# Layer 2 of a four-layer graph network: VectorE adds the four node chunks of a block's norm, and TensorE's sum over nodes takes one product per block

## The chip, the cores and the metric

The kernel runs on one core of a Trainium2 chip. The metric is the device time of one execution in microseconds, from the median of several runs. The profile is of one execution; its page and its trace give times in microseconds from the start of the span.

## The reference, cut to what matters

The program passes x, 8 batches of 2048 nodes with 64 features, through four layers. Each layer normalises its input over the features, takes the positive part h, and adds the layer's result on h to x:

```
h = maximum(layernorm(x), 0)
x = x + layer(h, adj)
```

Layers 0, 1 and 2 multiply h by the 2048 x 2048 matrix `adj` (once or more) and by small weights. Layer 3 is an attention over nodes whose scores are masked with `adj > 0.5`:

```
att = where(adj > 0.5, e, -9e15)
out = elu(einsum('bij,bjc->bic', softmax(att, axis=2), h))
```

Each row of `adj` is 0/1 divided by the row's sum, so with the given data an entry is usually far below 0.5, the mask is empty in every row, the softmax is uniform, and layer 3 is the mean of h over all nodes, through `elu`, added to x. The kernel computes this uniform case, tests on the way that the data allow it, and branches to a general path at the end if they don't. So for the last two layers, what is computed is: layer 2's result, added to x; its norm h; the sum of h over 2048 nodes for each batch and feature; `elu` of that sum divided by 2048, added to x.

## The kernel before, in words

The batches are taken in four pairs p. A pair's two batches lie side by side, so that a tile has 2 x 64 = 128 features. The nodes are taken in four blocks nb of 512, a block being four chunks of 128 nodes: a node block is a tile of 128 partitions by 4 chunks by 128 features. In layer 2 the blocks of all pairs are counted through as g = 4p + nb, from 0 to 15.

For each g, `product` (line 245) multiplies h, split into a high and a low half (tiles H and L), by the transposed pattern of `adj` (tile BT): 16 steps m of two matmuls each, into a bank of PSUM. VectorE then scales the bank into the tile e (`scaled`, line 240). The work of earlier blocks is hung between the steps of the product by the dictionary `fill`, whose keys are steps:

- at step 5, `behind(g)`: `finish2(g - 1)` multiplies e of block g - 1 by the layer's weights (`bn`, line 665), adds it to x (line 941, tile acc) and starts that block's norm;
- at step 12, `go_on`: the next stage of the norms that are under way;
- behind step 15, `sums(g - 2)`: TensorE multiplies a matrix of ones by the norm z of block g - 2, which sums z over its nodes (line 949, `pS`). Four products per block, one for each chunk, and all 16 products of a pair add up in one bank.

The norm (`norm_stages`, lines 174 to 200) goes over three engines: VectorE takes the mean and subtracts it (179 to 181), ScalarE squares (186), VectorE sums the squares (189, 191), GpSimd takes the power -1/2 (194), VectorE scales and takes the positive part (197). Then `done(h)` is called, which in layer 2 keeps z for `sums`.

After a pair's last block, `outputs` (from line 957) divides by the number of nodes, takes `elu` (960 to 963), adds it to the pair's four kept blocks (966) and stores them. Besides, `prepare_next` loads the next pair's h and splits it into H (ScalarE, line 230) and L (VectorE, line 232).

Behind the last product, `layer2` finishes block 15: `finish2(15)`, `sums(14)`, the rest of the norm, `sums(15)`, outputs.

The order of instructions on each engine is fixed when the kernel is built, by a planner that takes them in program order and moves some of them by its estimate of when their inputs are ready. Engines meet through semaphores.

Of the kernel before, what the change touches and what calls it, by code (L numbers as in the profile page):

```python
# [8 lines left out]
F32 = mybir.dt.float32  # L9
# [5 lines left out]
ALU = mybir.AluOpType  # L15
AX = mybir.AxisListType
# [26 lines left out]
def uniform_path(  # L43
# [30 lines left out]
    nc = tc.nc  # L74
    P = 128
    B, N, C = x.shape
    NP = B // 2
    NCH = N // P
    NB = N // 512
# [21 lines left out]
    def bank(tag, name):  # L101
        return psums[-1].tile([P, 512], F32, tag=tag, name=name)
# [11 lines left out]
    ones = consts.tile([P, P], F32, name="ones")  # L114
# [19 lines left out]
    def nodes(acc):  # L134

        return acc.rearrange("p j f -> p (j f)").rearrange("p (e j c) -> p j e c", e=2, c=C)
# [6 lines left out]
    def fill_x(acc, layer, p, nb, queue=nc.sync):  # L143
        if layer == 0:
            return queue.dma_start(runs(acc), runs_of(x, p, nb))
        return queue.dma_start(acc, xs[p][:, part(nb), :])
# [14 lines left out]
    def split(t):  # L161
        return t.rearrange("p j (b c) -> p j b c", b=2)
# [11 lines left out]
    def norm_stages(xt, name, done, out_):  # L174

        z = block("z", f"z_{name}", 3)
        g = groups(z)
        mean = small.tile([P, 8], F32, name="mean")
        nc.vector.tensor_reduce(each(mean), nodes(xt), axis=AX.X, op=ALU.add)
        nc.vector.tensor_scalar(mean, mean, 1.0 / C, None, op0=ALU.mult)  # L180
        firsts.append(nc.vector.tensor_tensor(  # L181
            split(z), nodes(xt), each(mean)[:, :, :, None].to_broadcast([P, 4, 2, C]),
            op=ALU.subtract
        ))
        sq = block("sq", f"sq_{name}", 1)
        squares.append(nc.scalar.activation(sq, z, AF.Square))  # L186
        yield
        var = small.tile([P, 8], F32, name="var", bufs=3)
        nc.vector.tensor_reduce(var, groups(sq), axis=AX.X, op=ALU.add)  # L189
        variances.append(  # L190
            nc.vector.tensor_scalar(var, var, 1.0 / C, EPS, op0=ALU.mult, op1=ALU.add)  # L191
        )
        rstd = small.tile([P, 8], F32, name="rstd", bufs=3)
        powers.append(nc.gpsimd.tensor_tensor(rstd, var, mhalf, op=ALU.pow))  # L194
        yield
        h = z if out_ is None else out_
        scales.append(nc.vector.scalar_tensor_tensor(  # L197
            groups(h), g, 0.0, rstd[:, :, None].to_broadcast([P, 8, C]), op0=ALU.max, op1=ALU.mult
        ))
        done(h)  # L200
        yield

    def norm_relu(xt, name, done, out_=None):
        n = norm_stages(xt, name, done, out_)
        next(n)
        pending.append([n, 2])
# [16 lines left out]
    lastp = []  # L223
# [52 lines left out]
    def term(k, name):  # L276
        pool = l0t if k == 1 else l0f[0]
        return pool.tile([P, 512], F32, tag=f"t{k}", name=name, bufs=(2, 4, 1)[k])
# [289 lines left out]
    for m in range(NCH):  # L568
        if m in (2, 7, 12):
            go_back(1 + m // 5)  # L570
        for i in range(2):
            nc.tensor.matmul(
                ps, hls[1][m // 4][i][:, m % 4, :], BT[:, m, 3 * 512:],
                start=(m == 0 and i == 0), stop=(m == NCH - 1 and i == 1),
# [80 lines left out]
    def feat(i, name):  # L655

        if i == 0:
            return term(1, name)
        return lastp[0].tile([P, 512], F32, tag="fm", name=name, bufs=4)

    def back_to_nodes(fT, wmat, name, tag="big"):

        ps = psums[-1].tile([P, 4, 2 * C], F32, tag=tag, name=f"bn_{name}")
        for t in range(4):
            nc.tensor.matmul(ps[:, t, :], fT[:, t * P:(t + 1) * P], wmat, start=True, stop=True)  # L665
        return ps
# [264 lines left out]
    accs, es, zs, pS = [], [], {}, {}  # L931

    def finish2(g):
        p, nb = divmod(g, NB)
        nm = f"acc_2_{p}_{nb}"
        acc = term(1, nm) if p % 2 else feat(1, nm)
        acc = acc.rearrange("p (j f) -> p j f", j=4)
        accs.append(acc)
        fill_x(acc, 2, p, nb)
        pn = back_to_nodes(es[g], wos, f"2_{p}_{nb}")  # L940
        nc.vector.tensor_tensor(nodes(acc), split(pn), nodes(acc), op=ALU.add)
        norm_relu(acc, f"3_{p}_{nb}", lambda h: zs.update({g: h}))

    def sums(g):
        p, nb = divmod(g, NB)
        if nb == 0:
            pS[p] = bank("tr", f"pS_{p}")
        for t in range(4):
            nc.tensor.matmul(  # L949
                pS[p][:, :2 * C], ones, zs[g][:, t, :],  # L950
                start=(nb == 0 and t == 0), stop=(nb == NB - 1 and t == 3),
            )
        if nb == NB - 1:
            outputs(p)

    def outputs(p):

        y = lastp[0].tile([P, 2 * C], F32, name="y")
        ex = lastp[0].tile([P, 2 * C], F32, name="ex")
        nc.vector.tensor_scalar(y, pS[p][:, :2 * C], 1.0 / N, None, op0=ALU.mult)  # L960
        nc.scalar.activation(ex, y, AF.Exp)
        nc.vector.tensor_scalar(ex, ex, 1.0, -1.0, op0=ALU.min, op1=ALU.add)
        nc.vector.scalar_tensor_tensor(y, y, 0.0, ex, op0=ALU.max, op1=ALU.add)
        for nb in range(NB):
            acc = accs[NB * p + nb]
            nc.vector.tensor_tensor(nodes(acc), nodes(acc), rows4(y), op=ALU.add)
            queue = nc.scalar if nb % 2 == 0 and p == NP - 1 else nc.sync
            queue.dma_start(runs_of(out, p, nb), runs(acc))

    def layer2(n, p):  # L970
        hl, _ = ops[n]

        def behind(g):
            go_on()
            if g > 0:
                finish2(g - 1)
            if g % NB > 1:
                prepare_next(n + 1, g % NB - 2)

        for nb in range(NB):  # L980
            g = NB * p + nb
            nm = f"2_{p}_{nb}"
            crow = load_crow(nb, nm)
            fill = {5: lambda: behind(g)}
            if g > 0:
                fill[12] = go_on
            if nb == 3:
                fill[8] = lambda: prepare_next(n + 1, 2)
            if g == 1:
                fill[9] = lambda: put_off.pop()()  # L990
            if g > 1:
                fill[15] = lambda: sums(g - 2)
            e = lastp[0].tile([P, 512], F32, tag="st", name=f"e_{nm}", bufs=3)
            es.append(product(hl, nb, nm, e, crow, fill=fill))
            if g == 0:
                go_on()
        prepare_next(n + 1, 3)
        if p == NP - 1:
            go_on()
            finish2(g)  # L1000
            sums(g - 1)
            all_done()
            sums(g)
# [600 lines left out]
```

## Time and profile before

The time before is 1248.38 us, the median of 3 runs (1244.74 to 1248.88). The profiled execution has a span of 1245.5 us.

| what | from the page or the trace |
|---|---|
| TensorE matmul busy | 1211.7 us, 97% of the span |
| VectorE busy | 745.5 us, 60% |
| ScalarE, GpSimd busy | 181.7 us (15%), 223.9 us (18%) |
| chain that ended last, by engine | TensorE 93%, DMA 3%, VectorE 3%, GpSimd 1% |
| `pS`, line 949: matmul records | 128, median 275 ns, from 1107.3 to 1235.6 us |
| granted TensorE clock, mean of the span | 0.994 |
| 1160 to 1170 us (layer 2, a block without outputs): VectorE busy | 4.97 of 10 us |
| 1170 to 1180 us (layer 2, a block with outputs): VectorE busy | 7.54 of 10 us |
| both of these: TensorE matmul busy | 10.00 of 10 us |

The page's chain is the way back from the last instruction, at each step to what released it or, where nothing did, to the instruction before it on its engine. An engine's share of the chain says how much of the end it set; its busy time alone doesn't. A product in 32-bit floats appears as two matmul records in the trace, so the four products of one block's sum are eight records. Matmuls overlap in the records (275 ns each, though eight of them take 0.89 us in the chain), so lengths on TensorE are read from the chain or from starts. TensorE is PE in the profile, its weight loads PEld, VectorE is DVE, ScalarE ACT, GpSimd POOL.

### The profile page before, as it was taken

To read this page: it belongs to the slowest core of one execution; us is meant where nothing else is said; L and a number is where in the kernel's file an instruction comes from. 1 tells how busy PE (TensorE), PEld (TensorE's weight loads), DVE (VectorE), ACT (ScalarE), POOL (GpSimd) and SP (SyncE) were. 2 spreads that over 40 slices of the span, in tenths; PEclk is the share of its full clock that TensorE was granted. 3 is DMA by queue.
4 is the path that set the end of the run, shared out by engine and by line. 5 is a ranking of instruction groups with operands and counts; after the bars stand their busy time and mean duration, and the time that the engine had idled before them with its cause. 6 is when DMAs were issued, how large, how long until landed. Compare 5 with 4: busy or idle time off the path is not lost.

```text
span 1245.5 us, 15336 instructions
## 1 busy us (share of the span) xinstructions
PE 1211.7 (97%) x5702; PEld 860.6 (69%) x5702; DVE 745.5 (60%) x1940; ACT 181.7 (15%) x281; POOL 223.9 (18%) x233
## 2 busy tenths in 40 slices
PE   5999999999999999999999999999999999999995
PEld 4775555555665557655577888788788878888884
DVE  5356888777757774477654445445543545566664
ACT  6610001000010000000111121112111211211100
POOL 5410222211131111011110022003101300231211
PEclk9999999999999999999999999999999999999998
DMA  9951334332332232122265436533643553433311
GB/s 358 372 142 53 101 107 115 85 87 72 90 106 67 65 89 79 51 64 64 60 148 135 110 100 153 116 90 119 161 106 90 152 127 96 128 137 117 115 56 46
DMA packets 100984, 140.98 MB, mean 113 GB/s; under 512 B 43772, under 2 KB 58108, under 8 KB 98852
## 3 DMA queue, kind: packets, MB, share of 16 engines
q1 hardware_dynamic: 82820, 80.74, 24.8%
q0 software_dynamic: 11776, 48.15, 13.0%
q10 hardware_dynamic: 6304, 11.01, 2.7%
q8 instruction: 47, 0.77, 0.2%
q14 instruction: 37, 0.30, 0.1%
HBM read 95.03 MB, written 35.66 MB: 105 GB/s over the span
## 4 chain that ended last, share of the span: by engine, by line
PE 93%; DMA 3%; DVE 3%; POOL 1%; issue 0%; ACT 0%; SPq 0%; POOLq 0%; ACTq 0%
PE bv L250 38%; PE y L711 26%; PE bn L665 5%; PE ph L900 3%; PE bv_2b L250 2%; PE bv_1b L250 2%; PE bv_3b L250 2%; PE bv_0b L250 2%; DMA BT<-in_adj_dram 2%; PE bn_u L665 1%; PE bv_0a L250 1%; PE bv_3a L250 1%; PE pt L262 1%; PE bv_2a L250 1%; PE pS L949 1%; PE bv_1a L250 1%
## 5 line engine op out<-in xcount | busy, mean ns | idle before, releaser
L250 PE MATMUL bv<-BT,H 128*128 128x512 f32 x1024 | 426.3, 416 | 0.0
L250 PE MATMUL bv<-BT,L 128*128 128x512 f32 x1024 | 401.0, 392 | 0.0
L250 PEld LDWEIGHTS bv<-BT,H 128*128 128x128 f32 x1024 | 192.5, 188 | 47.8 <-issue 11.6
L250 PEld LDWEIGHTS bv<-BT,L 128*128 128x128 f32 x1024 | 192.7, 188 | 47.5 <-issue 11.5
L720 DVE SCALAR_TENSOR_TENSOR acc<-y,emb,acc 128x128 f32<-128x128 f32 x512 | 176.2, 344 | 65.7 <-PE y L711 65.7
L720 DVE SCALAR_TENSOR_TENSOR odd<-y,emb,odd 128x128 f32<-128x128 f32 x448 | 153.3, 342 | 0.0
L711 PE MATMUL y<-wt,t0T 64*128 64x512 f32 x512 | 143.7, 607 | 2.4 <-DVE odd L720 1.7
L240 DVE TENSOR_TENSOR g<-bv,crow 128x512 f32<-128x512 f32 x48 | 33.2, 692 | 183.2 <-PE bv L250 183.2
L194 POOL TENSOR_TENSOR rstd<-var,mhalf 128x8 f32<-128x8 f32 x64 | 105.7, 1653 | 180.6 <-DVE var L191 174.8
L186 ACT ACTIVATE sq<-z 128x512 f32<-128x512 f32 x64 | 40.4, 631 | 406.6 <-DVE z L181 396.6
L711 PEld LDWEIGHTS y<-wt,t0T 64*128 64x128 f32 x512 | 45.8, 185 | 63.3 <-issue 57.1
L692 POOL TENSOR_TENSOR acc<-acc,b2r 128x512 f32<-128x512 f32 x16 | 22.2, 1389 | 315.5 <-DVE z L181 315.5
L692 POOL TENSOR_TENSOR acc<-acc,wl 128x512 f32<-128x512 f32 x16 | 20.7, 1291 | 299.3 <-DVE z L181 299.2
L711 PE MATMUL y<-wt,t1T 64*128 64x512 f32 x256 | 66.8, 589 | 0.0
L197 DVE SCALAR_TENSOR_TENSOR z<-z,rstd 128x512 f32<-128x512 f32 x64 | 44.7, 703 | 35.5 <-POOL rstd L194 35.5
L665 PEld LDWEIGHTS bn<-wl,g 128*128 128x128 f32 x384 | 49.5, 191 | 5.1 <-ACT g L905 1.5
L189 DVE TENSOR_REDUCE var<-sq 128x8 f32<-128x512 f32 x64 | 43.6, 681 | 15.6 <-ACT sq L186 15.6
L665 PE MATMUL bn<-wl,g 128*128 128x128 f32 x384 | 51.1, 276 | 0.0
L846 DVE SCALAR_TENSOR_TENSOR junk<-mt,cols,st 128x512 uint8<-128x512 bf16 x64 | 47.7, 745 | 4.1 <-DMA mt<-MD 3.7
L711 PEld LDWEIGHTS y<-wt,t1T 64*128 64x128 f32 x256 | 27.1, 187 | 27.8 <-issue 27.8
L905 ACT ACTIVATE g<-g,b1s 128x512 f32<-128x512 f32 x32 | 23.2, 724 | 137.2 <-DVE g L904 137.1
L691 POOL DMA_DIRECT2D hs<-z x32 | 18.6, 582 | 133.6 <-DVE z L197 97.0
(210 smaller groups left out, 1672.4 us busy)
## 6 DMA issues: line engine op xcount, KB each, us to landing
BT<-in_adj_dram POOLq DMA_DIRECT2D x16, 1024.0 KB, 19.5
crow<-crowD SPq DMA_DIRECT2D x64, 256.0 KB, 3.3
st<-in_adj_dram SPq DMA_DIRECT2D x64, 256.0 KB, 3.6
hs<-z POOLq DMA_DIRECT2D x40, 256.0 KB, 3.2
xs<-acc POOLq DMA_DIRECT2D x32, 256.0 KB, 2.4
MD<-BT POOLq DMA_DIRECT2D x16, 512.0 KB, 5.6
acc<-xs SPq DMA_DIRECT2D x32, 256.0 KB, 3.9
hb<-hs SPq DMA_DIRECT2D x28, 256.0 KB, 3.3
```

Source lines behind the costliest of these rows:

```text
L186: squares.append(nc.scalar.activation(sq, z, AF.Square))
L189: nc.vector.tensor_reduce(var, groups(sq), axis=AX.X, op=ALU.add)
L194: powers.append(nc.gpsimd.tensor_tensor(rstd, var, mhalf, op=ALU.pow))
L197: scales.append(nc.vector.scalar_tensor_tensor(groups(h), g, 0.0, rstd[:, :, None].to_broadcast([P, 8, C]), op0=ALU.max, op1=ALU.mult))
L240: ahead.append(nc.vector.tensor_tensor(to, ps.rearrange("p (q t) -> p t q", t=4), crow, op=ALU.mult))
L250: nc.tensor.matmul(ps, hl[m // 4][i][:, m % 4, :], BT[:, m, nb * 512:(nb + 1) * 512], start=(m == 0 and i == 0), stop=(m == NCH - 1 and i ...
L665: nc.tensor.matmul(ps[:, t, :], fT[:, t * P:(t + 1) * P], wmat, start=True, stop=True)
L692: nc.gpsimd.tensor_tensor(nodes(acc), nodes(acc), more, op=ALU.add)
L711: nc.tensor.matmul(y[:, bb, :], terms[k][hs_, ts], wt[hs_, k, dg * 512:(dg + 1) * 512], start=(k == 0), stop=(k == K - 1),)
L720: last = nc.vector.scalar_tensor_tensor(xj, yd, ec, old, op0=ALU.mult, op1=ALU.add)
L846: nc.vector.scalar_tensor_tensor(junk, mt, cols[:, i, :], st, op0=ALU.mult, op1=ALU.not_equal, accum_out=bad[:, i, q:q + 1],)
L900: fill[12] = lambda: nc.tensor.matmul(ph, w1v2 if s else w1vT, gT[nb], start=True, stop=True)
```

## The change

In blocks 0 to 14, VectorE adds the four chunks of z into one tile `hs4` of 128 partitions by 128 features as soon as the norm is done, and TensorE's sum takes that one tile: one product in place of four. Block 15 still gives its four chunks to TensorE. The purpose is to take work from TensorE, and to leave the last block's path as it is. The sum over nodes is the same but for the order of additions.

```
-        norm_relu(acc, f"3_{p}_{nb}", lambda h: zs.update({g: h}))
+        norm_relu(acc, f"3_{p}_{nb}", lambda h: add_chunks(g, h))
+
+    def add_chunks(g, h):
+
+        zs[g] = [h[:, t, :] for t in range(4)]
+        if g + 1 < NP * NB:
+            hs4 = lastp[0].tile([P, 2 * C], F32, name="hs4", bufs=2)
+            nc.vector.tensor_reduce(hs4, h.rearrange("p t f -> p f t"), axis=AX.X, op=ALU.add)
+            zs[g] = [hs4]
 
     def sums(g):
...
-        for t in range(4):
+        for t, z in enumerate(zs[g]):
             nc.tensor.matmul(
-                pS[p][:, :2 * C], ones, zs[g][:, t, :],
-                start=(nb == 0 and t == 0), stop=(nb == NB - 1 and t == 3),
+                pS[p][:, :2 * C], ones, z,
+                start=(nb == 0 and t == 0), stop=(nb == NB - 1 and t == len(zs[g]) - 1),
             )
```

## The prediction

> **What bounds the kernel now.** I read the page's chain by line first, then that chain in order of time over layer 2, then the timeline of VectorE alone over the same stretch, then the timeline of the last 27 us. Times inside the kernel are on the profile's clock.
>
> First, four blocks of layer 2 in the chain, in order of time (start, us, what). Each block is 12 + 20 matmuls of the large product, with the back-projection `bn` and the sum `pS` between them. The period is 1170.93 - 1161.86 = 9.07 us, made of 7.25 (32 large products at 0.227) + 0.91 (`bn`) + 0.91 (`pS`). No wait appears: TensorE bounds this stretch.
>
> ```profile
> 1161.86 0.89 PE pS L949 x8
> 1162.75 2.74 PE bv L250 x12
> 1165.49 0.89 PE bn L665 x8
> 1166.38 4.56 PE bv L250 x20
> 1170.93 0.89 PE pS L949 x8
> ```
>
> Second, VectorE in one of those blocks (start, us, then line, operation, tiles; in brackets idle time before it and its releaser). The reader is to see a serial circle: L941 takes `bn` in, its mean and centred tile go to ScalarE (0.76 us idle at L189), the variance to GpSimd (idle at L197), and only behind L197 does the next L941 stand. In a block with outputs, the next L941 is late because of L966.
>
> ```profile
> 1166.42 0.69 DVE L941 TENSOR_TENSOR acc<-bn,acc 128x512 f32<-128x512 f32 x1 [2.57 <-PE bn L665]
> ...
> 1168.07 0.69 DVE L181 TENSOR_TENSOR z<-acc,mean 128x512 f32<-128x512 f32 x1
> 1169.52 0.69 DVE L189 TENSOR_REDUCE var<-sq 128x8 f32<-128x512 f32 x1 [0.76 <-ACT sq L186]
> ...
> 1170.97 0.69 DVE L240 TENSOR_TENSOR e<-bv,crow 128x512 f32<-128x512 f32 x1 [0.56 <-PE bv L250]
> 1172.23 0.69 DVE L197 SCALAR_TENSOR_TENSOR z<-z,rstd 128x512 f32<-128x512 f32 x1 [0.56 <-POOL rstd L194]
> ...
> 1174.08 2.50 DVE L966 TENSOR_TENSOR acc<-acc,y 128x512 f32<-128x512 f32 x4
> 1176.50 0.68 DVE L941 TENSOR_TENSOR acc<-bn,acc 128x512 f32<-128x512 f32 x1
> ```
>
> Third, the tail in the chain: from 1227.35 the last block's L941, norm and sum are one serial path to the end at 1245.5, with no large product beside it.
>
> ```profile
> 1226.27 1.06 PE bn L665 x8
> 1227.33 0.02 issue
> 1227.35 0.70 DVE acc L941
> ...
> 1231.97 1.17 POOL rstd L194
> ```
>
> [...]the L941 at 1176.50 had its `bn` a microsecond earlier, and stood behind four L966.[...] No row of this trace has such a read: the reduces L179 and L189 read runs of 64 words.
>
> **The change part by part.**
>
> *Removed from TensorE.* In 15 of 16 blocks `pS` takes one product in place of four, that is 2 matmul records in place of 8. The remaining pair costs between 0.23 (a quarter of 0.91) and 0.40; the nearest pair, L861, added 0.31 (from the large product at 1081.33 to the second behind it at 1083.00 are 1.67 us, less two pitches, 0.45, and `bn`, 0.91). I take 0.27, so 0.64 per block. Blocks 0 to 12 lie in the stream: 13 x 0.64 = 8.3 us (6.6 to 8.8). Block 13's `pS` ends at 1226.27 beside the L240 of the last product (1225.41 + 0.69), for which `bn` waits anyway: 0. Block 14's lies in the tail's idle time: 0. Block 15 keeps four products.
>
> *Added to VectorE.* Fifteen reduces `hs4`, 128x128 out of 128x512, each reading four words 512 bytes apart, then stepping one word. Their length D is the unknown: 0.69 us if it reads as L189 does[...]. I take 0.69[...].
>
> *Where it stands.* In the build's order the reduce comes straight behind L197 and ahead of the next block's L941 (in two places per four blocks one or two other instructions move as well). So it is inside the circle. Behind it stand L941, then the whole norm, then L240, and TensorE's next `bn` waits for L240. The sum that reads `hs4` comes some 6 us later and waits for nothing.
>
> *The circle, worked out.* Without waits for TensorE, one turn is 1172.23 - 1166.42 = 5.81, plus the pitch of 0.61 to the next unrelated instruction: 6.42. From the L941 of block 1 (1105.28) to that of block 15 (1227.35) are 14 turns in 122.07 us. They need 14 x 6.42 = 89.9; plus the low halves L232 that lie between (ten of them, 0.6 each where visible: 2.2, 2.5 and 1.2 in the three groups of four) 5.9; plus three sets of outputs, 3.66 each now (1176.50 - 1172.84), about 3.1 in the new order, in which y is taken earlier and the exponential runs beside the reduce: 9.3; plus three places where the new order puts L240 ahead of L191, 0.6 each: 1.8. Sum 106.9, so the circle has 15.2 us to spare over the 14 turns. Each reduce takes D + 0.02 of it. The first one, in block 0, stands between L189 and L191 of layer 1's last norm at 1102.7 and moves the first L941 by D - 0.1. The last L941 moves by 14(D + 0.02) + (D - 0.1) - 15.2 = 15 D - 15.0 us. With D = 0.69 that is -4.7.
>
> *Which is later.* TensorE alone would be 8.3 us earlier, and the tail then pays block 14's reduce ahead of the last L941, +0.7: -7.6. The circle ends later, at -4.7, so it sets the end; TensorE waits for L240 in a few blocks (after product 2 first, where L240 ends only 1.0 us before `bn` starts even now: 1109.86 against 1110.89; then in the blocks with L232). The tail behind the last L941 is the same work. Buffers: z is freed earlier, the new tile has two buffers, no transfer is added: 0, all beside the products.
>
> **Forecast and rivals.** The median before is 1248.4.
> - *The reduce runs at full rate, the circle eats part of the gain* (0.48): 1248.4 - 4.7 = 1243.7.
> - *The strided read costs 1.04 us* (0.30): 15 x 1.04 - 15.0 = +0.6, that is 1249.0. The gain is turned into waits of TensorE's `bn` for L240.[...]
> - [...] (0.14): +3.0 to +6.6, at most 1255.0, slower than before; VectorE becomes the bound of layer 2.[...]
> - *TensorE stays the bound* (0.08): the circle is shorter than I summed (L232 and outputs slip into its idle time), -7.6, that is 1240.8.
>
> The range from 1240.0 to 1250.5 takes in three of the four and leaves out most of the third, some 0.15. Faster by over 0.3% (3.7 us): five sixths of the first case, as runs of one kernel scatter by 4 us (1244.74 to 1248.88), and the last: 0.40 + 0.08 = 0.48. Within 0.3%: the rest of the first, nearly all of the second, a little of the third: 0.37. Slower: 0.15.
>
> **What would show it.** Right: `hs4` rows of 0.68 to 0.70 us, 15 of them; `pS` pieces of about 0.27 in the chain; `bn` waiting for `e` of L240, about 2 us in all, first near 1110; VectorE entering the chain before 1220. D off: the `hs4` row says so at once, and each 0.1 us moves the end by 1.5. Wrong in the circle: no wait of `bn` for L240, and a period of 8.4 us throughout. Wrong on TensorE: a pair in `pS` that costs 0.5 or more.

## The result, and the profile after

In the first comparison the changed kernel took 1244.68 us (median of 4 runs, 1244.5 to 1245.27) and the kernel before 1247.76 (4 runs, 1244.74 to 1248.88): ratio 0.998, interval 0.9962 to 0.9998. In a second comparison of the same two kernels, with 13 runs against 35, it was 1245.88 against 1246.7, ratio 0.9998, interval 0.9989 to 1.0006. (The ratio is the recorded estimate from all runs; the two medians alone give 0.9993.) The first interval ends just under 1; the second, with far more runs, takes 1 in. So no gain is shown, and the second interval leaves one of 1.4 us at most (0.0011 x 1246.7).

To see where time goes inside layer 2, whole runs are too coarse, because runs of one kernel scatter by 4 to 5 us. From here on **the stretch** is the time from the first L240 of layer 2 (the `e` of block 0) to the first of the last four output additions. What follows it is the same work in every kernel. It takes 1237.28 - 1090.23 = 147.05 us before and 1235.00 - 1088.14 = 146.86 us after: 0.19 less. A second profile of the changed kernel (below) has 146.18, so two profiles of one kernel differ by up to 0.7 here, and 0.19 is within that.

The chain of waits after the change, by engine (section 4 of the page). It had 93% on TensorE before.

```profile
PE 86%; DVE 6%; DMA 3%; POOL 2%; issue 1%; ACT 1%; POOLq 0%; ACTq 0%; DVEq 0%
```

The chain of the changed kernel in order of time (start, us, what), at three places.

```profile
1123.47 0.22 PE pS L957 x2
1123.69 2.77 PE bv L250 x12
1126.46 0.89 PE bn L665 x8
1127.35 4.56 PE bv L250 x20
1131.91 0.22 PE pS L957 x2
...
1152.33 0.61 DVE var L189
...
1153.04 0.70 DVE e L240
...
1153.79 1.39 PE bn L665 x8
...
1188.49 1.65 POOL rstd L194
1190.16 0.70 DVE z L197
1190.88 1.07 DVE hs L949
1191.96 0.61 DVE acc L941
1192.59 0.70 DVE mean L179
```

First, TensorE's part of the gain is there: `pS` is 0.22 us in place of 0.89, and the period is 1131.91 - 1123.47 = 8.44 us in place of 9.07. Second, near 1153 `bn` comes behind L240 on VectorE: a wait that the kernel before did not have. Third, from there on pieces of VectorE's circle are in the chain, with the new addition (`hs`, L949) in the middle; no `bn` stands ahead of that L941.

VectorE alone after the change (start, us, line, operation, tiles; in brackets idle time before it and its releaser): a turn with outputs, then a plain one.

```profile
1165.04 0.69 DVE L941 TENSOR_TENSOR acc<-bn,acc 128x512 f32<-128x512 f32 x1 [0.34 <-PE bn L665]
...
1170.84 0.69 DVE L197 SCALAR_TENSOR_TENSOR z<-z,rstd 128x512 f32<-128x512 f32 x1 [0.36 <-POOL rstd L194]
...
1171.59 1.05 DVE L949 TENSOR_REDUCE hs<-z 128x128 f32<-128x512 f32 x1
...
1172.87 2.50 DVE L974 TENSOR_TENSOR acc<-acc,y 128x512 f32<-128x512 f32 x4
1175.29 0.68 DVE L941 TENSOR_TENSOR acc<-bn,acc 128x512 f32<-128x512 f32 x1
...
1190.88 1.07 DVE L949 TENSOR_REDUCE hs<-z 128x128 f32<-128x512 f32 x1
1191.88 0.68 DVE L941 TENSOR_TENSOR acc<-bn,acc 128x512 f32<-128x512 f32 x1
...
1199.40 0.68 DVE L941 TENSOR_TENSOR acc<-bn,acc 128x512 f32<-128x512 f32 x1
```

Two things are to be seen. The addition takes 1.05 to 1.07 us, where L189 reads as many elements in 0.69 (0.69 in the lines of the kernel before as well). And the L941 of blocks 1 to 15 have no idle time in brackets, but for one of 0.34: their `bn` is there already. Before, nine of the fifteen L941 of blocks 1 to 15 waited for `bn`, 14.9 us together. That idle time is what the addition has filled, and more: now TensorE waits (the waits of layer 2; who waited for whom, us in total, times, longest).

```profile
PEld bn L665 <- DVE e L240: 6.2, 5, 2.3
...
PE bn L665 <- DVE e L240: 4.4, 4, 1.9
```

### The profile page after: what moved, and what is told of

Same layout as the page of the kernel before. It is cut to its first block, busy times and chain, and to the rows that moved or that the text cites. A ratio compares the mean times of both kernels' runs of the same rounds, so it can differ in the third digit from the quotient of the medians.

```text
span 1243.5 us, 15171 instructions
## 1 busy us (share of the span) xinstructions
PE 1203.4 (97%) x5612; PEld 850.1 (68%) x5612; DVE 758.4 (61%) x1955; ACT 181.6 (15%) x281; POOL 223.8 (18%) x233
## 4 chain that ended last, share of the span: by engine, by line
PE 86%; DVE 6%; DMA 3%; POOL 2%; issue 1%; ACT 1%; POOLq 0%; ACTq 0%; DVEq 0%
PE bv L250 33%; PE y L711 26%; PE bn L665 4%; PE ph L900 3%; DMA BT<-in_adj_dram 3%; PE bv_3b L250 2%; PE bv_2b L250 2%; PE bv_1b L250 2%; PE bv_0b L250 2%; POOL rstd L194 1%; PE bn_u L665 1%; PE bv_0a L250 1%; PE bv_3a L250 1%; PE pt L262 1%; PE bv_2a L250 1%
## 5 line engine op out<-in xcount | busy, mean ns | idle before, releaser
L240 DVE TENSOR_TENSOR g<-bv,crow 128x512 f32<-128x512 f32 x48 | 33.2, 692 | 183.7 <-PE bv L250 183.7
L194 POOL TENSOR_TENSOR rstd<-var,mhalf 128x8 f32<-128x8 f32 x64 | 105.7, 1653 | 180.0 <-DVE var L191 174.2
L189 DVE TENSOR_REDUCE var<-sq 128x8 f32<-128x512 f32 x64 | 43.5, 680 | 15.6 <-ACT sq L186 15.6
```

The costliest lines, as they stand in the source:

```text
L240: ahead.append(nc.vector.tensor_tensor(to, ps.rearrange("p (q t) -> p t q", t=4), crow, op=ALU.mult))
```

## The experiments

Each kernel was timed beside the kernel before, in two sets: again, flat, one and four in the first, late, two, tree and pool in the second. Each has five runs or more. Each edit is in `add_chunks` unless said otherwise, and each diff is against the changed kernel. In the expectations, A is throughout the theory of the prediction with the length that was then measured: the serial circle on VectorE sets the end, and the addition is expensive because of its stride. The rivals look for the lost gain elsewhere: on TensorE, in a wait for the new tile, or in the shape of the addition rather than its stride.

| kernel | median us | ratio to before | stretch us | against before |
|---|---|---|---|---|
| changed kernel, again | 1245.88 | 0.9998 (0.9989 to 1.0006) | 146.18 | -0.87 |
| flat: neighbouring words | 1240.08 | 0.9951 (0.9938 to 0.9964) | 141.22 | -5.83 |
| one: no addition | 1237.84 | 0.9935 (0.9923 to 0.9947) | 138.81 | -8.24 |
| four: addition, not used | 1247.24 | 1.0006 (1.0000 to 1.0013) | 148.04 | +0.99 |
| late: addition moved | 1241.52 | 0.9960 (0.9946 to 0.9974) | 141.11 | -5.94 |
| two: halves, two products | 1241.03 | 0.9959 (0.9945 to 0.9972) | 141.61 | -5.44 |
| tree: two plain additions | 1240.34 | 0.9952 (0.9938 to 0.9966) | 140.54 | -6.51 |
| pool: the same on GpSimd | 1238.03 | 0.9939 (0.9926 to 0.9953) | 139.25 | -7.80 |

The kernel before was at 1246.7 in the first set and at 1246.47 in the second. The stretch is from one profile each, so differences of under 0.7 us in it say little. The medians tell the same story as the stretch: against the kernel before they fall by 6.6 us in flat, 8.9 in one and 8.4 in pool.

### again: the changed kernel once more

> The changed kernel once more, with more rounds, beside the kernel before on the same chip. In the first profiles the stretch of layer 2, from the first L240 of layer 2 to the last output add, was 146.86 us with the change against 147.05 before, 0.2 us shorter, while the medians stood 3.1 us apart. Theory A (the reduce of 1.07 us fills VectorE's circle, so the change gains nothing in layer 2; the rest of the difference lies in the first 20 us[...]): the stretch is again within 0.3 us of before, and the medians come closer, 0 to -2 us. Rival B (the change is truly worth 3 us somewhere): the medians stay 3 us apart.

Measured: 1245.88 us, -0.87 in the stretch. Of the 3.1 us of the first comparison 0.8 came back, and the interval takes in 1. Where the two profiled executions differ can be seen: their spans, 1245.5 and 1243.5 us, are 2.0 apart, and the difference lies ahead of layer 2, in code that is the same in all kernels. Whether the other runs of the first comparison differed there too isn't known, since only one of each kernel has a profile. TensorE's first stretches, before the change and then after it:

```profile
20.57 0.63 PE L479 MATMUL bv_1a<-BT,H 128*128 128x512 f32 x1
21.00 0.61 PE L479 MATMUL bv_2a<-BT,H 128*128 128x512 f32 x1
21.42 0.42 PE L479 MATMUL bv_0a<-BT,L 128*128 128x512 f32 x1
21.68 0.39 PE L479 MATMUL bv_1a<-BT,L 128*128 128x512 f32 x1
```

```profile
16.53 0.40 PE L479 MATMUL bv_1a<-BT,H 128*128 128x512 f32 x1
16.77 0.39 PE L479 MATMUL bv_0a<-BT,L 128*128 128x512 f32 x1
17.00 0.40 PE L479 MATMUL bv_1a<-BT,L 128*128 128x512 f32 x1
```

The pitch from one product to the next falls from 0.43 us to 0.23, at about 21.4 us in the one profile and 16.5 in the other. The first L240 of layer 2 starts at 1090.23 in the one and at 1088.14 in the other, 2.1 us earlier. Over the ten profiles of this study the pitch falls between 16.5 and 21.6 us. In the four that fall before 18 us that L240 starts between 1088.1 and 1088.8, in the other six between 1088.4 and 1090.9. What decides the moment was not tried.

### flat: the same addition without the stride

It adds four neighbouring words for each of the 128 results, in place of four words that lie 512 bytes apart: other elements, the same counts. Its sums are therefore not those of the reference.

```
-            nc.vector.tensor_reduce(hs4, h.rearrange("p t f -> p f t"), axis=AX.X, op=ALU.add)
+            runs4 = h.rearrange("p t f -> p (t f)").rearrange("p (f t) -> p f t", t=4)
+            nc.vector.tensor_reduce(hs4, runs4, axis=AX.X, op=ALU.add)
```

> The same number of reduces at the same place, each adding four neighbouring words in place of four words 512 bytes apart; the sums are of other elements, so layer 3's mean is not the reference's. Theory A (the length of the reduce comes from the stride, and each 0.1 us of it moves the end by 1.5): the reduce takes 0.69 us in place of 1.07, and layer 2 is 15 x 0.38 = 5.7 us shorter than with the change, some 141.2 us. Rival B (writing 128 results makes the reduce slow, not the stride): the reduce stays near 1.07 and the stretch near 146.9. Rival C (the reduce is long because of its stride, but VectorE's circle is not what sets the end): 0.69 us, and the stretch changes by under 1 us.

The addition in the costliest groups of VectorE over layer 2, in the changed kernel and then in flat (busy us, mean ns of one, idle us before it):

```profile
L949 DVE TENSOR_REDUCE hs<-z 128x128 f32<-128x512 f32 x15 | 15.9, 1062 | 0.3
```

```profile
L950 DVE TENSOR_REDUCE hs<-z 128x128 f32<-128x512 f32 x15 | 10.2, 683 | 0.3
```

It takes 683 ns in place of 1062 (the median is 1066), so it is the stride that costs 0.38 us, not the 128 results or the four-element sums. VectorE's instructions stand in the same order in both kernels, so no other place in the order can be the reason. The stretch is 5.64 us shorter than that of the changed kernel and 4.96 shorter than that of its second profile; 15 x 0.38 = 5.7. In these kernels a microsecond on VectorE at this place is very nearly a microsecond at the end.

### one: no addition at all

The first chunk alone goes to the sum; the other three are left out.

```
-            hs4 = lastp[0].tile([P, 2 * C], F32, name="hs4", bufs=2)
-            nc.vector.tensor_reduce(hs4, h.rearrange("p t f -> p f t"), axis=AX.X, op=ALU.add)
-            zs[g] = [hs4]
+            zs[g] = [h[:, 0, :]]
```

> TensorE's side of the change alone: blocks 0 to 14 give only their first chunk to the sum, with no reduce; three quarters of the nodes of these blocks are left out of layer 3's mean. Theory A (TensorE's gain is real and was given back by VectorE): 13 blocks x (0.91 - 0.22) = 9.0 us less than before, layer 2 near 138.0 us, no wait of bn for e. Rival B (TensorE's saving is smaller in the stream than the chain's pieces say): 4 us less or under.

The chain in one (start, us, what):

```profile
1123.76 0.22 PE pS L955 x2
1123.98 2.77 PE bv L250 x12
1126.75 0.89 PE bn L665 x8
1127.64 4.56 PE bv L250 x20
1132.20 0.22 PE pS L955 x2
```

Measured: -8.24 us in the stretch, ratio 0.9935. The period is 1132.20 - 1123.76 = 8.44 us, with no wait in it, and `bn` waits for L240 once in all of layer 2, 0.6 us behind the last product. The expectation of -9.0 took the difference of the pieces of `pS`, 0.69 us for a block; the period falls by 0.63 (from 9.07), and 13 x 0.63 = 8.2. So TensorE's saving is whole where nothing is added on VectorE: the removal of three products in four is worth 8.2 us, and the addition gives 7.4 to 8.1 of them back.

### four: the addition without its use

The addition is made, but TensorE keeps its four products.

```
             nc.vector.tensor_reduce(hs4, h.rearrange("p t f -> p f t"), axis=AX.X, op=ALU.add)
-            zs[g] = [hs4]
```

> VectorE's side alone: the reduces of the change are made, but TensorE still takes all four chunks of each block, and nothing reads the reduced tile. Theory A (the circle with the reduce in it is about as long as TensorE's stream before): layer 2 grows by 1 to 2 us, 1.1 of it the reduce of block 14 in the tail; bn waits for e in few places, under 2 us in all. Rival B (VectorE has room, as its busy share of 60 percent suggests): only the tail's 1.1 us, and no wait of bn for e.

Measured: +0.99 us in the stretch, and no wait of `bn` for L240. That is what rival B said: the tail's addition alone. VectorE in four, from the L941 of block 14 to that of block 15:

```profile
1219.38 0.69 DVE L941 TENSOR_TENSOR acc<-bn,acc 128x512 f32<-128x512 f32 x1
...
1225.19 0.69 DVE L197 SCALAR_TENSOR_TENSOR z<-z,rstd 128x512 f32<-128x512 f32 x1 [0.56 <-POOL rstd L194]
1225.91 1.05 DVE L949 TENSOR_REDUCE hs<-z 128x128 f32<-128x512 f32 x1
1226.88 0.68 DVE L941 TENSOR_TENSOR acc<-bn,acc 128x512 f32<-128x512 f32 x1
```

TensorE isn't later: from the L240 of block 0 to the `bn` of block 14 it takes 1218.45 - 1088.75 = 129.70 us, as before (1219.93 - 1090.23). The L941 of block 1 does start 0.85 us later (15.90 us behind the L240 of block 0 in place of 15.05), but VectorE's idle time takes that up. What reaches the end is block 14's addition, which stands ahead of the last L941: the two L941 shown are 7.50 us apart, where before it was 6.49 (1227.35 - 1220.86). So with TensorE's period at 9.07 us VectorE has room for the other 14 additions, if little: the L941 of blocks 1 to 15 still wait 2.7 us for `bn`, of 14.9 before. The addition alone costs 1 us, and what gives back 7 to 8 us in the changed kernel isn't the addition by itself but its meeting a TensorE that has become faster.

### late: the addition moved into VectorE's idle time

The addition is put behind the next block's L181, where VectorE waits 0.76 us for ScalarE's square.

```
+        if g - 1 in late:
+            add_late(g - 1)
...
+        late[g] = h
...
+    def add_late(g):
+        hs4 = lastp[0].tile([P, 2 * C], F32, name="hs4", bufs=2)
+        with tc.issue_after(firsts[-1].ins):
+            nc.vector.tensor_reduce(hs4, late[g].rearrange("p t f -> p f t"), axis=AX.X, op=ALU.add)
+        zs[g] = [hs4]
```

> The same strided reduce, moved behind the next block's L181, where VectorE waits 0.76 us for ScalarE's square; nothing else differs. Theory A (what costs is the place inside the circle): of its 1.07 us only some 0.35 lengthen a turn, the circle keeps 15.2 - 14 x 0.35 = 10.3 us to spare, TensorE sets the end again: layer 2 shorter than before by about 8.5 us, near 138.5. Rival B (VectorE is short of busy time as such): as with the change, near 146.9. Rival C (the sum now waits for a reduce that comes too late): TensorE's pS waits for it, several us in all.

Measured: -5.94 us, with an addition as long as ever (1075 ns). Most of the loss is gone by order alone. It falls short of -8.2, and here the sum has to wait once. TensorE in late (idle time and its releaser in brackets):

```profile
1109.25 0.49 PE L962 MATMUL pS<-hs,ones 128*128 128x128 f32 x2 [1.20 <-DVE hs L954]
```

That is 1.2 us; the chain has 0.48 to 0.49 us for the pair in place of 0.22 here and in three further blocks, another 1.1. From the L240 of block 0 to the `bn` of block 14 late takes 123.62 us (1214.49 - 1090.87) where one takes 121.46, so about 2.2 of the 2.3 us that it is behind one lie on TensorE, and these waits are of that size. In the last two blocks the addition lies on the serial path (0.99 and 0.94 us), but ScalarE's square runs beside it, and what is left of the difference behind that `bn` is 0.15 us.

### two: halves added on VectorE, two products left

```
-            hs4 = lastp[0].tile([P, 2 * C], F32, name="hs4", bufs=2)
-            nc.vector.tensor_reduce(hs4, h.rearrange("p t f -> p f t"), axis=AX.X, op=ALU.add)
-            zs[g] = [hs4]
+            nc.vector.tensor_tensor(h[:, 0:2, :], h[:, 0:2, :], h[:, 2:4, :], op=ALU.add)
+            zs[g] = zs[g][:2]
```

> VectorE adds the halves only (256 elements, 0.42 us), TensorE takes two products per block. Theory A: the circle moves by 15 x 0.45 - 15.0 = -8.2 us and TensorE by 13 x (0.91 - 0.45) = -6.0, plus 0.45 in the tail, so TensorE sets the end: layer 2 about 5.5 us shorter than before, near 141.5, better than the change although TensorE keeps more work. Rival B (the number of products on TensorE decides): worse than the change, which takes one product per block.

Measured: -5.44 us. It leaves TensorE twice the work of the changed kernel in the sum and yet ends 4.6 to 5.3 us earlier, since VectorE's addition is one of 128x256 with both sources in order (0.42 us on the mean, as expected). Here it matters less which engine's instruction is saved than what the circle is asked to carry.

### tree: the whole addition as two plain ones

The first line of two, and in place of its second:

```
+            nc.vector.tensor_tensor(h[:, 0, :], h[:, 0, :], h[:, 1, :], op=ALU.add)
+            zs[g] = zs[g][:1]
```

> VectorE adds in two contiguous steps inside z, halves (256 elements) and then quarters (128), one product per block as in the change.[...] Theory A (length times place): 15 x 0.77 - 15.0 = -3.4 us against before, layer 2 near 143.6. Rival B (two instructions that depend on each other cost as much as the one reduce): near 146.9.

VectorE in tree:

```profile
1212.83 0.43 DVE L948 TENSOR_TENSOR z<-z 128x256 f32<-128x256 f32 x1
1213.29 0.29 DVE L949 TENSOR_TENSOR z<-z 128x128 f32<-128x128 f32 x1
1213.50 0.68 DVE L941 TENSOR_TENSOR acc<-bn,acc 128x512 f32<-128x512 f32 x1
```

The two take 0.43 + 0.29 = 0.72 us and compute what the change's addition of 1.07 computes, but for the order of the four words. The expectation put in 0.77 us for the pair, an assumed length; from the start of the first to L941 are 1213.50 - 1212.83 = 0.67. The stretch is 6.51 us shorter than before, three more than expected; 1.5 of them are the circle that was summed too long (below). Most of the rest is order: the L941 of block 1 starts only 0.21 us later than before (15.26 us behind the L240 of block 0) where about 0.67 (0.77 - 0.1) was to come, the three turns with outputs are shorter than the change's by 0.55 us where a plain turn is by 0.32, as L971 fills the gap between the two additions, and in block 14 L941 stands between them, a turn of 6.87 us in place of 7.46.

### pool: the two plain additions on GpSimd

As tree, with `nc.gpsimd` in place of `nc.vector` in both lines.

> The two contiguous adds on GpSimd, which waits for VectorE most of the time; VectorE makes no reduce, TensorE takes one product per block. Theory A (VectorE's circle is free of the add): layer 2 as with TensorE's gain alone, 9 us shorter than before, near 138.0; it should beat both kernels. Rival B (GpSimd's adds, an estimated 0.7 and 0.4 us from its 1.29 for 512 elements, hold up its own power step in the circle, or slow VectorE down beside them): each turn grows by up to 1 us, and the gain falls to 0 to 4 us.

The chain in pool:

```profile
1123.20 2.77 PE bv L250 x12
1125.97 0.89 PE bn L665 x8
1126.86 4.56 PE bv L250 x20
1131.42 0.22 PE pS L957 x2
```

The same picture goes on from 1120 to 1165 without a gap, and `bn` waits 0.8 us in the whole layer: TensorE bounds it again, with its period of 8.44 us. Measured: -7.80 us, 1238.03 us in all, ratio 0.9939. But for 0.44 us in the stretch this is the kernel without any addition, and it is faster than both kernels of the case. It is not quite free. The additions on GpSimd (groups of pool: busy us, mean ns, idle before) and VectorE's four output additions in a block in which they run beside them:

```profile
L948 POOL TENSOR_TENSOR z<-z 128x256 f32<-128x256 f32 x15 | 13.0, 867 | 12.5 <-DVE z L197 8.0 <-DVE ex L970 2.7 <-PE bn L665 0.9
L949 POOL TENSOR_TENSOR z<-z 128x128 f32<-128x128 f32 x15 | 7.9, 527 | 1.2
```

```profile
1201.37 3.18 DVE L974 TENSOR_TENSOR acc<-acc,y 128x512 f32<-128x512 f32 x4
```

The four took 2.50 us in the changed kernel; here it is 3.18 in three blocks. VectorE has time to spare in this kernel (its L941 wait 7.7 us for `bn` in blocks 1 to 15), so little of it reaches the end.

## Why the prediction was right and where it was wrong

**The time lay in the range, but the likeliest case wasn't what happened.** The forecast of 1243.7 was 1248.4 - 4.7. Neither term held. The kernel before is at 1246.7 over 35 runs, so the base was 1.7 too high; and layer 2 became 0.2 to 0.9 us shorter, not 4.7. That the first median, 1244.68, came within 1 us of 1243.7 is luck. What happened is the second case, in which the strided read costs 1.04 us (1.07 measured) and TensorE's gain turns into waits of `bn` for L240.

**The step that failed: "I take 0.69".** The length D of the addition is 1.07 us (15 of them, 1019 to 1091 ns). Flat, with D = 0.683, shows what the step assumed, and 15 x 0.38 = 5.7 us is the whole of the mis-sized term. The nearest rows of before, L179 and L189, take 0.68 us on the mean for 512 elements, but they read runs of 64 words; that the addition would be as fast was assumed. The 1.04 of the second case, against 1.07 measured, was an assumption too and rested on no row of before. So the choice between the two had nothing measured behind it. One row came near: L240 reads its bank of PSUM with a step of four words at every element and takes 0.69 us, so "No row of this trace has such a read", one that steps over words at every element, is true of SBUF alone. Why the one step costs nothing and the other 0.38 us, no run here shows.

**The circle was right, and 1.5 us too long.** The prediction gave VectorE's 14 turns 106.9 us without the addition. Three profiles test it: take the time from the L941 of block 1 to that of block 15, less the idle time at L941, less 14 (D + 0.02). Changed kernel: 121.05 - 0.34 - 15.2 = 105.5. Its second profile: 120.37 - 0 - 15.2 = 105.2. Flat: 115.80 - 0.43 - 9.8 = 105.5. The turns tell which term it was. A plain turn is 7.5 us, that is 6.4 without the addition, as summed. A turn with outputs is 1175.29 - 1165.04 = 10.25, so 2.7 more than a plain one where 3.1 was taken: 1.1 over three turns. The remaining 0.3 to 0.6 are left for the terms of L232 and of the order of L240, which were not measured one by one.

With that the sum closes. 15 D - 15.0 is +1.0 with D = 1.066. The circle takes 1.4 off (105.5 for 106.9), the first step 0.1 (the L941 of block 1 moved by 15.90 - 15.05 = 0.85, and D - 0.1 is 0.97), and the 0.34 at L941 comes on top: -0.2, and -0.19 was measured. (The 105.5 is from the same profile, so this shows only that nothing is left over; the test is that flat gives 105.5 too.) The change breaks even at a D of about 1.08 to 1.12 us, so the case is a draw by the accident of the stride's price.

**TensorE.** This part was right. The pair's piece in the chain is 0.22 us, but the period says what it adds: 8.44 - 7.25 - 0.91 = 0.28, where 0.27 was taken. The 8.3 us over 13 blocks are seen where nothing holds them back (8.24 in one). "The tail behind the last L941 is the same work" holds: 8.65 us from there to the `y` of the last outputs, 8.67 before.

**What was to show it.** The first wait of `bn` for L240 came at product 2, near 1110 as said, and the longest in a block with L232 (TensorE in the changed kernel):

```profile
1108.68 1.16 PE L665 MATMUL bn<-wl,e 128*128 128x128 f32 x8 [0.37 <-DVE e L240]
...
1153.79 1.39 PE L665 MATMUL bn<-wl,e 128*128 128x128 f32 x8 [1.83 <-DVE e L240]
```

VectorE was in the chain before 1220. The waits of `bn` are 4.4 us in place of some 2, and that each 0.1 us of D moves the end by 1.5 is what flat shows (5.0 to 5.6 for 0.38).

**The other rivals.** "TensorE stays the bound" (-7.6) did not come for this kernel, and is what pool does (-7.8). The case of +3.0 to +6.6, with an addition longer still, falls with the measured length: the longest of the 15 took 1.09 us.

## What to carry to other kernels

An engine that is busy for 61% of the span, as VectorE is in the changed kernel, can set the end, if its work is a serial circle through other engines: count one turn of it, with its waits, against the period of the engine that bounds the kernel, before work is moved from the one to the other. Ask of moved work how it reads its data (here two plain additions cost 0.72 us and one strided reduce 1.07, for the same sums), and whether it can stand in an idle gap of its engine, as in late, or on another engine that has time to spare, as in pool (GpSimd has the power of L194 to do in the circle, but waits for VectorE most of the time: in the changed kernel 102.7 of the 155 us from 1088 to the end). Where runs scatter at the start by more than the effect, measure the stage that the change touches.

## What the runs showed of the hardware that I had not expected

- A `tensor_reduce` of 128x512 fp32 words into 128x128 takes 683 ns with four neighbouring words to a sum and 1062 ns with four words 512 bytes apart: 0.38 us, or 55%, for the stride alone.
- GpSimd adds 128x256 fp32 words in 0.87 us on the mean and 128x128 in 0.53, against 0.42 and 0.29 on VectorE (in tree). Single ones took 0.72 to 1.07 and 0.46 to 0.79. Four output additions of VectorE that coincide with them take 3.18 us in place of 2.50. That GpSimd's additions are what slows VectorE's is read from the coincidence; no run separates it.
- The moment at which TensorE's pitch falls from 0.43 to 0.23 us lies between 16.5 and 21.6 us after the start in ten profiles whose code is the same up to there. The start of layer 2 scatters by 2.8 us in the same profiles, and the two go together only in part.
